# Six constants behind the first gates, three state copies on VectorE, and new delays in the planner of a two-layer macaron kernel

## The chip, the cores and the metric

The kernel runs on one core of a Trainium2 chip. A core has five engines with an instruction stream each: TensorE (PE; its weight loads are listed as PEld), VectorE (DVE), ScalarE (ACT), GpSimd (POOL) and SyncE (SP), which issues most of the transfers. Each engine runs its own instructions strictly in program order and waits for the others by semaphores. The metric is the device time of one execution in microseconds (us), lower is better.

## The reference

The input is x of 8 batches by 256 positions by 128 channels, 2048 tokens in all. The model is six residual steps, each on the layer norm of x:

```python
x = x + 0.5 * ffn0(layernorm(x))      # top 2 of 8 experts, 128 -> 512 -> 128, relu
x = x + attn0(layernorm(x))           # recurrence over 256 positions
x = x + 0.5 * ffn0(layernorm(x))      # the same experts again
x = x + 0.5 * ffn1(layernorm(x))      # 8 experts of 256, gelu, one expert for a token
x = x + attn1(layernorm(x))           # 16 heads, relu scores
x = x + 0.5 * ffn1(layernorm(x))
```

The recurrence of attn0 keeps an 8 by 8 state M for each batch and head (128 of them, one for each partition), with q and k scaled to unit length:

```python
out_t = einsum('bnh,bnhd->bnd', q_t, M)
delta = v_t - einsum('bnhd,bnd->bnh', M, k_t)
M = M + b_t * einsum('bnh,bnd->bnhd', k_t, delta)
```

Its output is divided by its root mean square, multiplied by rms_weight, and projected by Wo.

## The kernel before

**Tokens.** x lies in SBUF as 16 tiles of 128 tokens; a tile is 16 positions of all 8 batches. The first three steps run over five chunks of tiles, CHUNKS = (first tile, number): (0,3), (3,4), (7,4), (11,3), (14,2). So chunk 0 has 48 positions, chunks 1 and 2 have 64, chunk 3 has 48 and chunk 4 has 32.

**Calls of the first FFN.** There are eight, named by a pair: ("in",0) and ("in",1) for chunks 0 and 1, ("in",2) for the other nine tiles at once, and ("out",0) to ("out",4), which are the third step, a call for each chunk. ("in",0) and ("out",4) run every expert over all their tokens ("dense"); the rest are sorted. Below they are written in0 to in2 and out0 to out4; the profile joins names that differ in a number alone, so that pypin is the second projection of in1 and in2.

A call's path: `layer_norm` (L253; statistics on VectorE L259, reciprocal root on GpSimd L250, scaling on ScalarE L268); transposes on TensorE (ptg, L343) and gates (L323; logits plg, softmax with an exponential ex on ScalarE, the two best experts by VectorE, `both` L377). Then, for a sorted call, `route` (L423): TensorE counts the tokens of each expert (pcr, L444 and behind), VectorE makes each token's place (`slot`, L478) and each tile's expert (`tei`, L491), and `scattering` (L497) sends the rows to a buffer in DRAM, one indirect transfer by GpSimd for each tile and choice (L506): 18 for in2, 8 for out1. SyncE loads each tile's expert weights (`loading`) and fetches the sorted rows four tiles at a time (`fetching`, L714, xs). `experts` (L722) transposes them (ptp, L739), multiplies (ph, L793; py, L770), and stores the results as rows. `combining` (L813) gathers the rows for each token by GpSimd (yg, L864), weights them on ScalarE (dg, by half_ident), sums them on TensorE (pbc, L838 and L841) and adds them to x (L849). Before it TensorE turns the gates (pgb, L399).

**The scan.** `prepare` (L880) makes k, v, q and the rates of a chunk: layer norm, projections (pps, L929), activations (sps, L907), two transfers through DRAM that turn the layout (dts and ts), and `inverse` (L932), which squares on ScalarE (sqs, L937), sums on VectorE (sss, L940, sms, L944), takes the root (nrs, L947) and the reciprocal (nes, ris, L950 and L953). For each tile of the chunk it then copies v into the last column of a buffer of 16 states (M, L991, on ScalarE). `steps` (L1012) walks through the positions on VectorE in six instructions each (rk, L1054; u, L1059; e, L1032; Ms, L1064; r, L1068; mk, L1037). For each finished tile `finish` (L1080) multiplies states by q on GpSimd (qmo, L1094; q's own scaling, qns, is L1002) and sums on TensorE (pmo, L1100); once the chunk is done it turns the layout by DRAM (do, ot), takes the root mean square (pro, L1122; veo and rso, L247 and L250), projects by woT (pwo, L1130) and adds to x. A chunk's scan needs the state of the one before.

**What sets the order.** Nothing is scheduled by a compiler: each engine's program order is the order in which the class `Weave` (L43) emits. Streams (Python generators) say what they want next: an engine with an estimate of its time and the lag until its result is there, or a key that somebody has to mark. `Weave` keeps a time for each engine at which it is free, emits the earliest possible item (of items equally early the one of the higher rank) and moves the times on. A mark may be set later than now: `routed` (L511) is marked 2.5 us after the last scatter, `fetched` (L719) 3.0 us after its transfer's issue. An item of GpSimd between 1.25 and 1.35 us, that is a scatter or a gather, pushes VectorE's time back by 0.5 (L102). All these numbers act on the emitted order; at run time the engines wait for semaphores.

**Constants.** They are made before the streams start: half_ident (L139), part (L161 to L164, from two iotas), woT times rms_w (L207) and before (L215), six instructions on VectorE. half_ident is read by `combining`, before by `route`, woT by pwo, part by the second attention.

Of the kernel before, what the change touches and what calls it, by code (L numbers as in the profile page):

```python
# [17 lines left out]
P = 128  # L18
B, S, D = 8, 256, 128
NH, HD = 16, 8  # L20
E = 8
# [21 lines left out]
class Weave:  # L43
# [17 lines left out]
    def mark(self, key, us=None):  # L61
        self.done[key] = self.now if us is None else us
# [8 lines left out]
    def run(self, streams):  # L71
        for rank, s in streams:
            self.spawn(s, rank)
        streams, at, nexts = self.streams, self.at, self.nexts
        while any(n is not None for n in nexts):
            best = None
            for i, n in enumerate(nexts):
                if n is None:
                    continue
                if n[0] in self.free:  # L80
                    start = max(at[i], self.free[n[0]])
                elif n[0] == "until":
                    start = max(at[i], n[1])
                elif n in self.done:
                    start = max(at[i], self.done[n])
                else:
                    continue
                if best is None or (start, -self.ranks[i], at[i]) < best[:3]:
                    best = start, -self.ranks[i], at[i], i
            if best is None:  # L90
                raise RuntimeError([(st.__name__, n) for st, n in zip(streams, nexts) if n])
            start, _, _, i = best
            self.rank = self.ranks[i]
            if nexts[i][0] in self.free:
                engine, us, lag, table = nexts[i] + (None, None, LAGS[nexts[i][0]], None)[len(nexts[i]) :]
                if table and table != self.table:
                    self.load(table)
                    self.table = table
                    us += 1.3
                self.free[engine] = start + us  # L100
                if engine == "pool" and 1.25 < us < 1.35:
                    self.free["dve"] += 0.5  # L102
                start += us + lag
            at[i] = self.now = start
            nexts[i] = next(streams[i], None)
# [3 lines left out]
def kernel(ctx: ExitStack, tc: tile.TileContext, a: dict, out: bass.AP):  # L109
# [26 lines left out]
    ident = const.tile([P, P], F32, name="ident")  # L136
    make_identity(nc, ident)
    half_ident = const.tile([P, P], F32, name="half_ident")
    dve.tensor_scalar(half_ident, ident, 0.5, None, ALU.mult)  # L139
    ones = const.tile([P, P], F32, name="ones")  # L140
    pool.memset(ones, 1.0)
    mean_col = const.tile([P, 1], F32, name="mean_col")
# [15 lines left out]
    pool.iota(row, pattern=[[0, 4]], base=0, channel_multiplier=1)  # L158
    col = const.tile([P, 4], I32, name="col")
    pool.iota(col, pattern=[[1, 4]], base=0, channel_multiplier=0)  # L160
    dve.tensor_scalar(row, row, 3, 3, ALU.logical_shift_right, ALU.bitwise_and)  # L161
    part = const.tile([P, 4], F32, name="part")
    dve.tensor_tensor(part, row, col, ALU.is_equal)
    dve.tensor_scalar(part, part, QSCALE, None, ALU.mult)  # L164

    x1 = const.tile([P, NT, D], F32, name="x1")

# [9 lines left out]
    def slots_of(n, k=2):  # L177

        return (k * n * P + E * (P - 1)) // P
# [13 lines left out]
    def woven(dram, moe, pools):  # L193
# [5 lines left out]
        xd = dram.tile([B, S, D], F32, name="xd", tag="xd", bufs=1)  # L199
        n_f = F0 // P  # L200
        n_c = len(CHUNKS)
        tile_no = const.tile([P, slots_of(NT)], F32, name="tile_no")
        pool.iota(
            tile_no, pattern=[[1, slots_of(NT)]], base=0, channel_multiplier=0,
            allow_small_or_imprecise_dtypes=True,
        )
        dve.tensor_scalar(woT, woT, rms_w, None, ALU.mult)  # L207

        before = const.tile([E, 2, E], F32, name="before")
        pool.memset(before, 1.0)  # L210
# [1 line left out]
            out=before[:, 1, :], in_=before[:, 1, :], compare_op=ALU.is_ge, fill=0.0, base=0,  # L212
            pattern=[[1, E]], channel_multiplier=-1,
        )
        dve.tensor_scalar(before[:, 0, :], earlier[:E, :E], float(P), None, ALU.mult)  # L215


        calls = {("in", c): CHUNKS[c] for c in (0, 1)}
# [13 lines left out]
        for i in range(2):  # L232
            sorted_tiles[f"f{i}"] = slots_of(SORTED, 1)
            places[f"f{i}"] = 2 + i
            rooms.append(slots_of(SORTED, 1))

        def vec(n):

            return "dve", 0.07 + 0.00105 * n, 0.14

        SQRT, SILU, EXP, GELU = (f"{f}_and_others" for f in ("sqrt", "silu", "exp", "gelu"))

# [254 lines left out]
        def scattering(key, slots):  # L497
            c = chosen[key]
            n = sizes[key]
            yield "clear", places[key]  # L500

            views = dram_disjoint_views(dram_of[key][0], len(slots) * n)
            for i in range(n):
                for k in range(len(slots)):
                    yield "pool", 1.3, 0
                    pool.indirect_dma_start(  # L506
                        out=views.pop(),
                        out_offset=bass.IndirectOffsetOnAxis(ap=slots[k][:, i : i + 1], axis=0),
                        in_=c["xn"][:, i, :], in_offset=None,
                    )  # L510
            mark(("routed", key), weave.now + 2.5)  # L511

        def dram_rows(i, nt):

# [188 lines left out]
        def fetching():  # L703

            k = 0
            for key, nt in sorted_tiles.items():
                yield "routed", key
                for t in range(0, nt, TB):
                    if k >= XB:
                        yield "turned", k - XB  # L710
                    yield "sp", 0.4, 0
                    m = min(TB, nt - t)
                    xs = moe.tile([P, TB, D], F32, name=f"xs{k}", tag="xs", bufs=XB)
                    sync.dma_start(  # L714
                        out=xs[:, :m],
                        in_=dram_of[key][0][t * P : (t + m) * P].rearrange("(q p) d -> p q d", p=P),
                    )
                    sources[key, t // TB] = xs, m
                    mark(("fetched", key, t // TB), weave.now + 3.0)  # L719
                    k += 1  # L720

        def experts(key):  # L722
# [157 lines left out]
        def prepare(c):  # L880
# [104 lines left out]
            for i in range(n):  # L985
                if t0 + i >= MB:
                    yield "summed", t0 + i - MB
                yield "act", 0.35
                M = scan.tile([P, SL, HD, HD + 1], F32, name=f"M{name}_{i}", tag="M", bufs=MB)
                vs = v.rearrange("p h t -> p t h")[:, i * SL + 1 : min((i + 1) * SL + 1, ct)]  # L990
                act.copy(M[:, : vs.shape[1], :, HD], vs)  # L991
                states[t0 + i] = M
                mark(("room", t0 + i))
                if i == 0:
                    weave.spawn(queries(c, q, inverse))
# [10 lines left out]
        def scanning():  # L1006
            last = None
            for c in range(n_c):
                yield "room", CHUNKS[c][0]
                last = yield from steps(c, last)  # L1010

        def steps(c, last):  # L1012
# [33 lines left out]
            for t in range(ct):  # L1046
                if t and t % SL == SL - 1 and t + 1 < ct:
                    yield "room", t0 + t // SL + 1
                more = t + 1 < ct
                if more:  # L1050
                    yield "dve", 0.09, 0.0
                    rk = small.tile([P, HD], F32, name=f"rk{c}_{t}", tag="rk")
                    dot = small.tile([P, 1], F32, name=f"dot{c}_{t}", tag="dot")
                    dve.tensor_tensor_reduce(  # L1054
                        rk, r, kn[:, t + 1, :HD], 1.0, 0.0, ALU.mult, ALU.add, dot
                    )
                yield "dve", 0.14, 0.0
                u = small.tile([P, HD, HD], F32, name=f"u{c}_{t}", tag="u")
                dve.tensor_tensor(u, bc(kb[:, t], HD), bc_mid(r, HD), ALU.mult)  # L1059
                if more:  # L1060
                    yield "dve", 0.14, 0.0
                    e = e_of(t, mk)
                yield "dve", 0.13, 0.0
                dve.tensor_tensor(M(t + 1)[:, :, :HD], M(t)[:, :, :HD], u, ALU.add)  # L1064
                if more:
                    yield "dve", 0.08, 0.05
                    r = small.tile([P, HD], F32, name=f"r{c}_{t + 1}", tag="r")
                    dve.scalar_tensor_tensor(r, kb[:, t], dot, e, ALU.mult, ALU.add)  # L1068
                if t + 2 < ct:
                    yield "dve", 0.15, 0.0  # L1070
                    mk = mk_of(t + 1, t + 1)
                if t % SL == SL - 1:
                    mark(("states", t0 + t // SL))
            return end

        def finishing():
            for c in range(n_c):
                yield from finish(c)

        def finish(c):  # L1080
# [23 lines left out]
            yield "sp", 0.4, 2.8  # L1104
            do = dram.tile([P, HD, ct], F32, name=f"do{name}", tag=f"do{ct}")
            sync.dma_start(out=do, in_=o)
            yield "sp", 0.4, 2.8
            ot = scan.tile([P, BW], F32, name=f"ot{name}", tag="ot", bufs=1)
            ot = ot[:, : n * P].rearrange("p (b t) -> p b t", b=B)
            sync.dma_start(out=ot, in_=do.rearrange("(b n) d t -> (n d) b t", b=B))  # L1110
# [30 lines left out]

        def routing():
            for key in calls:
                if key[0] == "out":
                    yield "finished", key[1]
                    if key[1] > 1:
                        yield "x", ("out", key[1] - 2)
                yield from gates(key)
# [575 lines left out]
        def attended(b, sums):  # L1724
# [33 lines left out]
            for qc in range(2):  # L1758
# [16 lines left out]
        weave.run(  # L1775
            [
                (1, loading()), (1, fetching()), (1, routing()), (1, tensor()), (2, adds()), (2, combines()),
                (0, scanning()), (3, preparing()), (2, finishing()), (2, moving()), (1, clearing()),
                (1, opening()), (3, heads("f0")), (-1, everyone("f0")), (1, experts("f0")), (2, returning("f0")),
                (3, projecting()), (1, scoring()), (2, weighing()),  # L1780
                (3, heads("f1")), (-1, everyone("f1")), (1, experts("f1")), (2, returning("f1")), (1, storing()),
# [73 lines left out]
```

## Time and profile before

| | us |
|---|---|
| median of 9 runs | 871.78 |
| lowest to highest | 868.23 to 874.84 |
| profiled execution, its own time | 872.66 |
| its span, first to last instruction | 870.9 |
| mean granted TensorE clock | 0.889 |
| scan steps of chunk 0 | 99.3 to 147.3 |
| chunk 1 | 173.1 to 246.1 |
| chunk 2 | 254.8 to 325.5 |
| chunk 3 | 328.5 to 377.1 |
| chunk 4 | 380.9 to 422.2 |
| TensorE on in2's experts | 114.1 to 192.8 |
| TensorE on out1's experts | 314.8 to 363.5 |
| first tile of out2's experts | 403.5 |

The rows of chunks are the first and the last scan step on VectorE, with other instructions of VectorE between the steps. After out2 come out3, out4 and the second layer, some 450 us, in which TensorE leads most of the time.

The profile lists for each instruction its start from the beginning of the span, its duration, engine, line, operation and tiles; in square brackets stands the idle time of the engine just before it and what ended that. "POOL rsgin <- DVE vegin" is a wait of GpSimd for VectorE. The chain follows the work that ended last back to its releaser, piece by piece.

### The profile page before, as it was taken

To read this page: it belongs to the slowest core of one execution; us is meant where nothing else is said; L and a number is where in the kernel's file an instruction comes from. 1 tells how busy PE (TensorE), PEld (TensorE's weight loads), DVE (VectorE), ACT (ScalarE), POOL (GpSimd) and SP (SyncE) were. 2 spreads that over 40 slices of the span, in tenths; PEclk is the share of its full clock that TensorE was granted. 3 is DMA by queue.
4 is the path that set the end of the run, shared out by engine and by line. 5 is a ranking of instruction groups with operands and counts; after the bars stand their busy time and mean duration, and the time that the engine had idled before them with its cause. 6 is when DMAs were issued, how large, how long until landed. Compare 5 with 4: busy or idle time off the path is not lost.

```text
span 870.9 us, 17110 instructions
## 1 busy us (share of the span) xinstructions
PE 714.9 (82%) x5236; PEld 582.5 (67%) x5236; DVE 541.0 (62%) x3186; ACT 419.1 (48%) x1036; POOL 241.9 (28%) x337
## 2 busy tenths in 40 slices
PE   3999879986997558755999898995999999999581
PEld 2888868874586458744998786663955556666481
DVE  2434696398879999987501413768276876467721
ACT  3456737751476327512566444331566565554130
POOL 1041751017514430353323300003052332300303
PEclk9999979985699569866999997996999999999876
DMA  8075845605352455225495201005110000000522
GB/s 303 1 234 120 227 127 139 190 29 161 93 152 65 113 178 135 77 82 149 134 309 148 71 12 29 0 1 161 37 35 2 2 1 2 1 1 1 152 59 69
DMA packets 102842, 82.77 MB, mean 95 GB/s; under 512 B 38816, under 2 KB 82080, under 8 KB 102752
## 3 DMA queue, kind: packets, MB, share of 16 engines
q1 hardware_dynamic: 97840, 71.30, 28.4%
q0 software_dynamic: 4480, 9.18, 3.5%
q10 hardware_dynamic: 432, 1.20, 0.4%
q8 instruction: 43, 0.70, 0.3%
q14 instruction: 47, 0.39, 0.2%
HBM read 57.79 MB, written 23.86 MB: 94 GB/s over the span
## 4 chain that ended last, share of the span: by engine, by line
PE 53%; DVE 32%; DMA 4%; POOL 4%; issue 3%; ACT 3%; SPq 1%; POOLq 0%; ACTq 0%; DVEq 0%
PE ps L1665 4%; PE pa L1709 4%; DVE u L1059 4%; PE phpin L793 3%; DVE r L1068 3%; PE phf L1457 3%; DVE mk L1037 3%; PE pypin L770 3%; DVE Ms L1064 3%; PE pyf L1475 3%; PE phdin L664 3%; PE pypout L770 3%; PE phpout L793 3%; DVE e L1032 3%; PE pydin L674 2%
## 5 line engine op out<-in xcount | busy, mean ns | idle before, releaser
L1475 PEld LDWEIGHTS pyf<-w_W,hf 128*128 128x128 f32 x512 | 70.7, 200 | 24.9 <-issue 21.4
L1475 PE MATMUL pyf<-w_W,hf 128*128 128x128 f32 x512 | 76.0, 287 | 2.8 <-DVE x L1512 2.8
L797 ACT ACTIVATE hpout<-phpout,w 128x128 f32<-128x128 f32 x224 | 63.6, 372 | 30.0 <-PE phpout L793 26.5
L1464 ACT ACTIVATE hf<-phf 128x512 f32<-128x512 f32 x64 | 38.2, 597 | 64.9 <-PE phf L1457 64.9
L1457 PE MATMUL phf<-xTf,w_W 128*128 128x512 f32 x128 | 68.6, 621 | 0.0
L1059 DVE TENSOR_TENSOR u<-kbs,r 128x64 f32<-128x64 f32 x256 | 64.0, 250 | 0.2
L770 PE MATMUL pypout<-W,hpout 128*128 x448 | 60.4, 279 | 3.9 <-ACT hpout L797 3.9
L793 PE MATMUL phpout<-xTpout,w 128*128 128x128 f32 x448 | 60.3, 279 | 1.6 <-ACT xTpout L743 1.4
L1068 DVE SCALAR_TENSOR_TENSOR r<-kbs,dot,e 128x8 f32<-128x8 f32 x251 | 61.0, 243 | 0.0
L1037 DVE TENSOR_TENSOR mk<-Ms,kns 128x72 f32<-128x72 f32 x251 | 57.0, 227 | 5.5 <-ACT Ms L991 5.5
L770 PEld LDWEIGHTS pypout<-W,hpout 128*128 128x128 f32 x448 | 55.3, 194 | 4.7 <-ACT hpout L797 4.3
L1064 DVE TENSOR_TENSOR Ms<-Ms,u 128x64 f32<-128x64 f32 x251 | 57.3, 228 | 0.0
L793 PEld LDWEIGHTS phpout<-xTpout,w 128*128 128x128 f32 x448 | 55.5, 195 | 2.5 <-ACT xTpout L743 2.0
L797 ACT ACTIVATE hpin<-phpin,w 128x128 f32<-128x128 f32 x160 | 45.5, 378 | 18.4 <-PE phpin L793 12.8
L1032 DVE TENSOR_REDUCE e<-mk 128x8 f32<-128x72 f32 x251 | 53.5, 213 | 0.0
L1681 DVE TENSOR_SCALAR w<-ps 128x512 f32<-128x512 f32 x64 | 42.6, 683 | 15.7 <-PE ps L1665 15.4
L1094 POOL TENSOR_TENSOR qmo<-Ms,qns 128x1024 f32<-128x1024 f32 x16 | 32.0, 1999 | 67.0 <-DVE r L1068 50.0
L1100 PE MATMUL pmo<-qmo,ident 128*128 128x128 f32 x256 | 41.8, 332 | 6.2 <-POOL qmo L1094 6.0
L793 PE MATMUL phpin<-xTpin,w 128*128 128x128 f32 x320 | 45.5, 289 | 1.6 <-ACT sps L907 0.9
L1665 PE MATMUL ps<-q,k 32*128 32x256 f32 x512 | 45.4, 404 | 1.7 <-DVE w L1681 1.4
L1678 ACT ACTIVATE w<-ps 128x512 f32<-128x512 f32 x64 | 35.8, 596 | 22.5 <-PE ps L1665 22.1
L506 POOL DMA_INDIRECT rows<-xnf,slotrf x16 | 16.0, 997 | 109.2 <-DVE pastrf L482 104.9
(362 smaller groups left out, 1721.3 us busy)
## 6 DMA issues: line engine op xcount, KB each, us to landing
w<-in_w_dram SPq DMA_DIRECT2D x112, 258.0 KB, 3.4
xs<-rows SPq DMA_DIRECT2D x27, 256.0 KB, 3.6
rows<-x SPq DMA_DIRECT2D x5, 768.0 KB, 5.3
w<-in_w_dram SPq DMA_DIRECT2D x30, 128.0 KB, 2.5
rows<-ypout SPq DMA_DIRECT2D x12, 256.0 KB, 2.5
rows<-ypin SPq DMA_DIRECT2D x9, 256.0 KB, 2.3
W<-in_w_dram SPq DMA_DIRECT2D x8, 256.0 KB, 5.4
w_W<-in_w_dram SPq DMA_DIRECT2D x8, 256.0 KB, 4.8
```

The lines of the kernel that those rows point to most:

```text
L770: pe.matmul(py[:, t % TB, :], lhsT=h[:, g, :], rhs=of(e, g), start=g == 0, stop=g == n_f - 1)
L793: pe.matmul(ph[:, f, :], lhsT=first(w, f), rhs=xT[:, t % TB, :], start=True, stop=True)
L797: act.activation(h[:, f, :], ph[:, f, :], AF.Relu, bias=bias(w, f))
L1032: dve.tensor_reduce(e, mk, AX.X, ALU.add)
L1037: dve.tensor_tensor(mk, M(t), bc_mid(kn[:, t + 1], HD), ALU.mult)
L1059: dve.tensor_tensor(u, bc(kb[:, t], HD), bc_mid(r, HD), ALU.mult)
L1064: dve.tensor_tensor(M(t + 1)[:, :, :HD], M(t)[:, :, :HD], u, ALU.add)
L1068: dve.scalar_tensor_tensor(r, kb[:, t], dot, e, ALU.mult, ALU.add)
L1457: pe.matmul(ph, lhsT=l1["W"][:, e, f * P : (f + 1) * P], rhs=c["xT"][k], start=True, stop=True,)
L1475: pe.matmul(py[:, i, :], lhsT=before[0][ff][:, i * P : (i + 1) * P], rhs=second1(before[3], ff), start=ff == 0, stop=ff == n_f - 1,)
L1665: pe.matmul(pss[g][0][:, kc, :], lhsT=k[rows, j, kc * P : (kc + 1) * P], rhs=q[rows, :], start=True, stop=True,)
L1681: dve.tensor_scalar(w, ps, 0.0, None, ALU.max)
```

## The change

It has three parts.

1. The six constant instructions on VectorE leave the start. A new stream, `constants`, of rank 2 emits them once the gates of in0 have been emitted, and the routing waits for it before the gates of in1.
2. The copies of v into the state buffers of chunk 0, three of them, go to VectorE. Those of the other chunks stay on ScalarE.
3. Numbers of the planner: an indirect transfer pushes VectorE's time back by 0.8 instead of 0.5; routed is marked 4.0 after the last scatter instead of 2.5; fetched 4.5 after the issue instead of 3.0; the transfer of ot has a lag of 4.2 instead of 2.8; three of a scan step's six costs go from 0.13, 0.08 and 0.15 to 0.135, 0.1 and 0.17. The helper `vec` moves up so that the new stream can use it.

```diff
                 if engine == "pool" and 1.25 < us < 1.35:
-                    self.free["dve"] += 0.5
+                    self.free["dve"] += 0.8
...
-    dve.tensor_scalar(half_ident, ident, 0.5, None, ALU.mult)
...
-    dve.tensor_scalar(row, row, 3, 3, ALU.logical_shift_right, ALU.bitwise_and)
     part = const.tile([P, 4], F32, name="part")
-    dve.tensor_tensor(part, row, col, ALU.is_equal)
-    dve.tensor_scalar(part, part, QSCALE, None, ALU.mult)
...
-        dve.tensor_scalar(woT, woT, rms_w, None, ALU.mult)
...
-        dve.tensor_scalar(before[:, 0, :], earlier[:E, :E], float(P), None, ALU.mult)
+        def constants():
+
+            yield "gates", ("in", 0)
+            yield vec(E)
+            dve.tensor_scalar(before[:, 0, :], earlier[:E, :E], float(P), None, ALU.mult)
+            yield vec(P)
+            dve.tensor_scalar(half_ident, ident, 0.5, None, ALU.mult)
+            yield vec(P)
+            dve.tensor_scalar(woT, woT, rms_w, None, ALU.mult)
+            yield vec(4)
+            dve.tensor_scalar(row, row, 3, 3, ALU.logical_shift_right, ALU.bitwise_and)
+            yield vec(4)
+            dve.tensor_tensor(part, row, col, ALU.is_equal)
+            yield vec(4)
+            dve.tensor_scalar(part, part, QSCALE, None, ALU.mult)
+            mark(("constants",))
...
-            mark(("routed", key), weave.now + 2.5)
+            mark(("routed", key), weave.now + 4.0)
...
-                    mark(("fetched", key, t // TB), weave.now + 3.0)
+                    mark(("fetched", key, t // TB), weave.now + 4.5)
...
-                yield "act", 0.35
+                yield vec(SL * HD) if c == 0 else ("act", 0.35)
                 M = scan.tile([P, SL, HD, HD + 1], F32, name=f"M{name}_{i}", tag="M", bufs=MB)
                 vs = v.rearrange("p h t -> p t h")[:, i * SL + 1 : min((i + 1) * SL + 1, ct)]
-                act.copy(M[:, : vs.shape[1], :, HD], vs)
+                (dve.tensor_copy if c == 0 else act.copy)(M[:, : vs.shape[1], :, HD], vs)
...
-                yield "dve", 0.13, 0.0
+                yield "dve", 0.135, 0.0
                 dve.tensor_tensor(M(t + 1)[:, :, :HD], M(t)[:, :, :HD], u, ALU.add)
                 if more:
-                    yield "dve", 0.08, 0.05
+                    yield "dve", 0.1, 0.05
...
-                    yield "dve", 0.15, 0.0
+                    yield "dve", 0.17, 0.0
...
-            yield "sp", 0.4, 2.8
+            yield "sp", 0.4, 4.2
             ot = scan.tile([P, BW], F32, name=f"ot{name}", tag="ot", bufs=1)
...
+                if key == ("in", 1):
+                    yield ("constants",)
...
-                (0, scanning()), (3, preparing()), (2, finishing()), (2, moving()), (1, clearing()),
+                (0, scanning()), (3, preparing()), (2, constants()), (2, finishing()), (2, moving()), (1, clearing()),
```

In the order that comes out each engine has the instructions it had, but for the three copies and for three more loads of ScalarE's activation tables (23 instead of 20): two around the exponential of in2's gates, one around that of out1's.

## The prediction

> **What bounds the kernel now.** I read the page's shares and its chain first, then the timelines of the engines that the moved work touches, then the stretch in which TensorE stands still.
>
> ```profile
> PE 714.9 (82%) x5236; PEld 582.5 (67%) x5236; DVE 541.0 (62%) x3186; ACT 419.1 (48%) x1036; POOL 241.9 (28%) x337
> PE 53%; DVE 32%; DMA 4%; POOL 4%; issue 3%; ACT 3%; SPq 1%; POOLq 0%; ACTq 0%; DVEq 0%
> ```
>
> TensorE and VectorE share the path: TensorE through the experts, VectorE through the scan, and they hand over by gathers and scatters on GpSimd (POOL). So what counts is which instruction stands ahead of which on each engine; nothing is added but three VectorE instructions in ScalarE's stead, and three table loads.
>
> **The start.** VectorE's timeline opens with the constants:
>
> ```profile
> 8.40 0.29 DVE L207 TENSOR_SCALAR w_rows<-w_rows 128x128 f32<-128x128 f32 x1 [8.40 <-DMA w_rows<-in_rows_dram]
> ...
> 9.28 0.15 DVE L215 TENSOR_SCALAR before<-earlier 8x8 f32<-8x8 f32 x1
> 9.36 0.28 DVE L259 BATCH_NORM_STATS2 stgin<-x 128x6 f32<-128x128 f32 x1
> ```
>
> The first statistics stand behind L207, whose rows land at 8.40, though ScalarE's first table load at 4.05 is released by x itself. With the six constants gone they start at 4.05: gain 9.36 − 4.05 = 5.3 us. TensorE, whose transposes follow, is busy 30.0 of 30 us from 20 to 50, so it hands the gain on; w1, which the first expert matmul at 15.71 needs, landed at 9.05 and would be needed at 10.4. Bounds: 0, if a weight is late, to 5.3; I take 5.3. The constants themselves (0.96 us) go behind the first gates.
>
> **State copies.** L991 takes 432 ns on ScalarE. On VectorE no such copy exists; a 128x1 copy (L1356) takes 149 ns, a 128x256 one (L1641) 421, and the nearest, 128x128 (L1329), 291. Three are 0.4 to 1.3 us, and I take 0.8 on VectorE against up to the 1.92 that it waited for ScalarE's copy before chunk 0. Neither counts: after chunk 0 the scan stands still for its next input.
>
> ```profile
> 147.37 1.87 DVE L1064 TENSOR_TENSOR end<-Ms,u 128x64 f32<-128x64 f32 x1
> 159.85 0.69 DVE L940 TENSOR_REDUCE sss<-sqs 128x64 f32<-128x512 f32 x1 [10.61 <-ACT sqs L937]
> 246.27 0.68 DVE L940 TENSOR_REDUCE sss<-sqs 128x64 f32<-128x512 f32 x1
> ```
>
> The last line is chunk 2's norm: the squares it waits for ended at 244.07, so 2.2 us of slack lie there.
>
> **Planner numbers.** They issue nothing, but the whole order is built from them. Going through the new order engine by engine with the old durations, these moves matter.
>
> (a) The sorted tokens of in2. Chunk 0's sums, sms, nes and ris stand ahead of slotrin2 on VectorE, its matmuls pcrin2 stand later on TensorE, and exgin2 is behind two sps activations and one table load on ScalarE. On the old clock the slots come at 92.0 instead of 85.3: +6.7. Bounds: 3.4 (the three norm instructions and the activations alone) to 10.
>
> (b) GpSimd. Eighteen scatters (L506) run one by one, then eight gathers ygcin1 (L864):
>
> ```profile
> 85.31 1.03 POOL L506 DMA_INDIRECT rows<-xngin,slotrin  x1 [16.12 <-DVE terin L488]
> ...
> 108.30 0.96 POOL L506 DMA_INDIRECT rows<-xngin,slotrin  x1 [0.30 <-issue]
> 109.56 0.99 POOL L864 DMA_INDIRECT ygcin<-rows,slotrin  x1 [0.30 <-issue]
> ```
>
> In the new order the last four scatters stand behind all eight gathers. At 109.56 − 108.30 = 1.26 each that is +10.1. qns0 stands five scatters earlier, ahead of its input; I take 1.7 for that wait (0 to 3). The chain shows who waits:
>
> ```profile
> 108.30 2.27 DMA rows<-xngin,slotrin
> ...
> 110.64 3.44 DMA xs<-rows
> 114.07 0.04 issue
> 114.12 1.13 PE ptpin L739 x4
> ```
>
> All of in2's experts wait for the last scatter. Together 6.7 + 10.1 + 1.7 − 5.3 = +13.2: ptpin2_0 at 127.3 instead of 114.1.
>
> (c) TensorE around it. Moved ahead of that transpose, into the wait: pgbin1, two pbcin1 and pmo0_0, 6.9 us. Moved in before in2's last matmul: pmo1_0 and pmo1_1, 3.6. A new wait for out0's gate sums: 4.0 (0 to 6.5, the wait that pcrout had), while the old 3.4 at that place and 2.0 of small waits go. Sum −6.9 + 3.6 + 4.0 − 3.4 − 2.0 = −4.7. So in2's last matmul ends 13.2 − 4.7 = 8.5 late.
>
> (d) From there to the scan. A second out0 scatter stands ahead of gathers ygcin2 (+1.3), so chunk 2's tokens are +9.8, and after the 2.2 of slack the scan of chunk 2 starts +7.6. Chunk 1, whose preparation moves well ahead, starts some 10 us earlier, which gains nothing while chunk 2 waits for tokens. From chunk 2 on the scan carries the 7.6.
>
> (e) out1 and out2. slotrout1 moves six steps earlier (step 26 of chunk 2 instead of 32); at 0.77 us a step out1's tiles start 4.6 earlier against the scan, 310.2 on the old clock. But the eight gathers ygcout1 now stand ahead of rsgout2:
>
> ```profile
> 356.83 1.01 POOL L250 TENSOR_TENSOR rsgout<-vegout,minus_half 128x4 f32<-128x4 f32 x1 [6.11 <-DVE vegout L247]
> ...
> 367.99 1.05 POOL L864 DMA_INDIRECT ygcout<-rows,slotrout  x1 [0.17 <-issue]
> ```
>
> The gathers need out1's rows. out1's matmuls took 314.84 to 363.5, 48.7 us; without pwo2, pmo3_0 (3.3) and a wait of 3.5 for the last relu they end at 310.2 + 41.9 = 352.1; rows stored 2.9 later; gathers 10.1; then rsgout2: done at 366.1. VectorE wants it at 359.9 (offgout2, step 32 of chunk 3 in both orders). So the scan may stall 6.2, 9.7 if the relu's wait stays, or nothing if the rows come early. I take the middle of 0 and 9.7: +4.9. Then out2's slots stand six scan steps later (+4.6), rso3 in the middle of its scatters (+0.9), and pmo4_0, ptgout3 and plgout3 (3.7) run in TensorE's wait before out2 instead of in it: +1.8. After out2's middle TensorE's order is the old one.
>
> **Sum.** 7.6 + 4.9 + 1.8 = +14.3 against the profiled execution's 872.7: 887.0. That execution is 0.9 above the median of the nine runs, 871.8, so 886.
>
> **Two rules weighed, beside the sum.** Table loads: the trace's cost 1283 ns each, three more 3.8 us on an engine at 48%, covered by waits; the next activation follows 10 ns after a load. The Trainium skill ("ScalarE: Activation LUTs", section "What ACT_TABLE_LOAD costs") puts a drain of some 1380 ns on top, so three would be 8.0 us by it: it speaks against this change, but the trace shows no such drain, and I leave both out of the sum.
>
> While TensorE stood still its clock was granted less (columns: us, PE, PEld, DVE, ACT, POOL busy, granted clock, DMA share, GB/s):
>
> ```profile
> 100.00:110.00 10.00, 5.16 (x47) 4.97 (x45) 9.55 (x78) 4.36 (x15) 7.74 (x9) 0.90 0.75 206
> 110.00:120.00 10.00, 5.21 (x23) 4.56 (x24) 10.00 (x72) 2.00 (x7) 8.15 (x8) 0.50 0.52 152
> ```
>
> It was 0.50 from 108.0 to 121.7, 7.6 us into the work again: 3.8 us lost. "TensorE: Matmul & The Clock Gate" ("Part 1: The HAM clock gate") says that one idle window of about 3.4 us halves the rate and as much steady work restores it; by that the longer pause costs about the same once, by the row 3.8 once. In the sum it stays as it was.
>
> **The rivals.**
>
> R1, faster: the start gain carries. If GpSimd's slots come early enough that ptpin2_0 runs by 112.6 and out1's rows come early enough for rsgout2, the rest of the sum (−1.5 to there, −4.7, +1.3, −2.2, +1.8) gives −5.3, the start's own gain: 871.8 − 5.3 = 866. For it: a TensorE that hands on every early microsecond, its shortened stage, a chunk 1 that starts earlier. Against: the ten microseconds of gathers in a queue that is full, as its 0.30 us gaps show. By the same terms it turns where ptpin2_0 comes at 117.9.
>
> R2, no change: (a) at its lower bound (−3.3), no wait of qns0 (−1.7), none of out0's gate sums (−4.0) and none at offgout2 (−4.9): 886 − 13.9 = 872. Each is possible, all four together are not likely, though one early start of the scatters would help three of them.
>
> R3, much slower: the same queue at its worst. rsgout2 with the full stall of 9.7 (+4.8), and in2's slots at the upper bound (+3.3): 886 + 8 = 894. It needs out1's tail unshortened.
>
> R4: the numbers do not do what they say, that is, later marks move order alone and the transfers land as before (xs in 3.2 us median, scatter in 2.27). That is true of every mark, and is why no gain is put down to them: it is a part of each case.
>
> **How the numbers follow.** Main case 0.47 (878 to 890 as its own range), R1 0.26, R2 0.13, R3 0.14. Changes under 0.3%, 2.6 us, cannot be told from none. Faster: R1 and a little of R2, 0.28; same: most of R2, 0.09; slower 0.63. The range goes from 863, R1 with 3 more from the earlier chunk 1, to 893, just under R3.
>
> **What would show it.** bn_stats at about 4.1; the first slotrin2 scatter after 85 and four scatters behind the gathers; ptpin2_0 near 127; chunk 2's scan starting near 262; an idle stretch on VectorE at offgout2 of about 5; out2's scatters some 14 later than 385.8. If ptpin2_0 comes before 118, or the stall at offgout2 is absent while chunk 2 starts no later than 255, the forecast is wrong.

## The result, and the profile after

| | before | after |
|---|---|---|
| median, us | 871.78 | 892.93 |
| lowest to highest | 866.79 to 875.82 (31 runs) | 891.23 to 897.08 (10 runs) |
| span of the profiled execution | 870.9 | 892.1 |
| mean granted TensorE clock | 0.889 | 0.874 |

The change makes the kernel slower: ratio 1.025, 95% interval 1.0228 to 1.0273. The forecast had 886 and the direction; but the way there differs, and its second half was not foreseen. Setting each milestone of the two traces side by side shows it (start of the first, end of the last instruction, us):

| milestone | before | after | forecast shift | measured shift |
|---|---|---|---|---|
| first statistics | 9.4 | 4.1 | -5.3 | -5.2 |
| in2's slots (end of slotrin2) | 84.5 | 85.3 | +1.4 | +0.8 |
| in2's first transposes | 114.1 | 127.3 | +13.2 | +13.2 |
| in2's last matmul | 192.8 | 197.7 | +8.5 | +4.9 |
| first step of chunk 2's scan | 254.8 | 258.0 | +7.6 | +3.2 |
| out2's first transposes | 403.5 | 415.9 | +18.0 | +12.4 |
| out2's last matmul | 444.9 | 451.3 | +14.3 | +6.5 |
| first expert matmul of f0 | 519.4 | 533.5 | +14.3 | +14.1 |
| first scores of the second attention | 630.6 | 645.0 | +14.3 | +14.4 |
| first expert matmul of f1 | 746.6 | 768.8 | +14.3 | +22.2 |

So of the 21 us some 3 are there when chunk 2's scan begins, 6.5 at out2's end, 14.4 when the attention begins, and 22 when it is over. Between f0 and the attention, where TensorE's order is the same in both traces, the shift stays (14.1 and 14.4). Lines of after are 12 higher than those of before from the new stream on, 14 in the second layer, and in the kernels with a recorded order higher again. GpSimd's timeline of after around in2:

```profile
86.06 1.11 POOL L518 DMA_INDIRECT rows<-xngin,slotrin  x1 [22.45 <-DVE pastrin L494]
...
97.70 1.13 POOL L1014 TENSOR_TENSOR qns<-ts,ris 128x384 f32<-128x384 f32 x1 [1.66 <-DVE mk L1049]
...
106.81 0.98 POOL L876 DMA_INDIRECT ygcin<-rows,slotrin  x1 [0.49 <-issue]
...
115.60 0.94 POOL L876 DMA_INDIRECT ygcin<-rows,slotrin  x1 [0.30 <-issue]
116.85 1.00 POOL L518 DMA_INDIRECT rows<-xngin,slotrin  x1 [0.30 <-issue]
...
120.69 0.96 POOL L518 DMA_INDIRECT rows<-xngin,slotrin  x1 [0.30 <-issue]
```

Eight gathers stand between the fourteenth and the last four scatters, and qns0 waits 1.66 us. TensorE's timeline shows what was done in the pause and when in2 begins:

```profile
109.51 0.77 PE L853 MATMUL pbcin<-ygcin,dgcin 128*128 128x128 f32 x2 [5.34 <-DMA ygcin<-rows,slotrin]
...
123.70 3.78 PE L1112 MATMUL pmo<-qmo,ident 128*128 128x128 f32 x16 [4.67 <-POOL qmo L1106]
127.28 1.06 PE L751 MATMUL ptpin<-ident,xs 128*128 128x128 f32 x4
129.01 2.05 PE L805 MATMUL phpin<-xTpin,w 128*128 128x128 f32 x16 [0.67 <-ACT xTpin L755]
```

The windows over in2's experts, before's first, then after's (columns as in the prediction):

```profile
114.12:192.80 78.68, 72.59 (x540) 66.62 (x540) 57.73 (x402) 52.00 (x152) 16.99 (x13) 0.91 0.45 123
```

```profile
127.28:197.70 70.42, 65.42 (x530) 61.47 (x530) 66.65 (x495) 49.55 (x146) 11.22 (x7) 0.97 0.46 129
```

in2 takes 8.3 us less. A part of it is work that was moved into the pause, another the clock, 0.97 instead of 0.91: of in2's stretch 13.8 us ran at 0.50 in before and 4.8 in after. Work at half clock now lies in the pause, ahead of in2 (pmo0_0 took 3.78 us for 16 matmuls there, against 1.95 in before).

The late stretch, on GpSimd, VectorE and TensorE of after:

```profile
498.75 0.94 POOL L876 DMA_INDIRECT ygcout<-rows,slotrout  x1 [0.30 <-issue]
499.71 2.04 POOL L262 TENSOR_TENSOR rsf<-vef,minus_half 128x4 f32<-128x4 f32 x2
```

```profile
500.79 0.36 DVE L1300 TENSOR_SCALAR xnf<-x,mvf,rsf 128x128 f32<-128x128 f32 x1 [6.34 <-POOL rsf L262]
501.05 0.35 DVE L707 SCALAR_TENSOR_TENSOR x<-pydout,gategout,x 128x128 f32<-128x128 f32 x1
```

```profile
501.45 2.07 PE L686 MATMUL pydout<-W,hdout 128*128 128x128 f32 x8 [4.19 <-DVE x L707]
```

The roots rsf00 and rsf01 of the second layer's first norm run behind all six gathers ygcout3; in before they ran behind four, at 491.02. VectorE takes its work in order, so the sums of the dense out4 (L707) wait behind the norm that needs rsf, and TensorE waits 4.19 us for a bank, a piece of the memory that it writes to, that these sums free. In before TensorE waited there too, for xnf, but 2.69 us. The windows show the clock behind it, before's first:

```profile
490.00:500.00 10.00, 7.01 (x34) 6.04 (x35) 3.46 (x13) 1.69 (x4) 5.05 (x5) 0.83 0.11 28
500.00:510.00 10.00, 10.00 (x73) 8.81 (x73) 1.97 (x6) 5.08 (x13) 0.00 (x0) 1.00 0.08 17
```

```profile
500.00:510.00 10.00, 8.55 (x33) 7.63 (x34) 3.11 (x12) 1.94 (x5) 1.75 (x2) 0.53 0.03 8
510.00:520.00 10.00, 10.00 (x49) 9.03 (x49) 1.68 (x5) 2.62 (x6) 0.00 (x0) 0.61 0.09 20
```

With the clock at 0.61 TensorE looks busy for all of the ten microseconds and does 49 matmuls, where before's does 73 at 1.00. Over the whole way from out2's last matmul to the first of f0, before's first:

```profile
444.87:519.42 74.55, 68.47 (x499) 62.30 (x498) 14.85 (x70) 41.97 (x117) 18.62 (x87) 0.98 0.40 125
```

```profile
451.34:533.47 82.13, 74.30 (x498) 67.67 (x497) 14.68 (x70) 42.23 (x117) 18.50 (x87) 0.90 0.35 101
```

Of the 7.6 us 5.8 are TensorE's own time for the same matmuls and 1.8 its idle time. Its clock was 0.50 for 17.1 us of that way, in before for 3.4; half of the difference, 6.8 us, is an estimate of what the clock cost.

### The profile page after: what moved, and what is told of

Same layout as the page of the kernel before. It is cut to its first block, busy times and chain, and to the rows that moved or that the text cites. A ratio compares the mean times of both kernels' runs of the same rounds, so it can differ in the third digit from the quotient of the medians.

```text
span 892.1 us, 17122 instructions
## 1 busy us (share of the span) xinstructions
PE 723.9 (81%) x5236; PEld 586.8 (66%) x5236; DVE 536.4 (60%) x3189; ACT 423.6 (47%) x1036; POOL 241.0 (27%) x337
## 4 chain that ended last, share of the span: by engine, by line
PE 49%; DVE 29%; POOL 7%; issue 6%; ACT 4%; DMA 4%; SPq 0%; POOLq 0%; DVEq 0%; ACTq 0%
DVE x L1526 4%; PE ps L1679 4%; PE pa L1723 3%; PE phf L1471 3%; PE phdin L676 3%; PE phpout L805 3%; PE pmo L1112 3%; PE pypout L782 3%; DVE u L1071 3%; PE pyf L1489 3%; PE pydin L686 2%; PE pypin L782 2%; DVE mk L1049 2%; DVE Ms L1076 2%; PE phpin L805 2%
## 5 line engine op out<-in xcount | busy, mean ns | idle before, releaser
L1112 PE MATMUL pmo<-qmo,ident 128*128 128x128 f32 x256 | 45.1, 349 | 22.2 <-POOL qmo L1106 17.1
L1071 DVE TENSOR_TENSOR u<-kbs,r 128x64 f32<-128x64 f32 x256 | 60.6, 237 | 0.1
L1112 PEld LDWEIGHTS pmo<-qmo,ident 128*128 128x128 f32 x256 | 42.5, 259 | 24.8 <-POOL qmo L1106 18.5
L1080 DVE SCALAR_TENSOR_TENSOR r<-kbs,dot,e 128x8 f32<-128x8 f32 x251 | 57.0, 227 | 0.0
L809 ACT ACTIVATE hpin<-phpin,w 128x128 f32<-128x128 f32 x160 | 45.5, 374 | 17.1 <-PE phpin L805 12.4
L1066 DVE CUSTOM_DVE_ANT_0 rk<-r,kns 128x8 f32<-128x8 f32 x251 | 45.7, 182 | 0.1
## 6 DMA issues: line engine op xcount, KB each, us to landing
w<-in_w_dram SPq DMA_DIRECT2D x112, 258.0 KB, 3.6
```

What stands on the lines that cost most here:

```text
L809: act.activation(h[:, f, :], ph[:, f, :], AF.Relu, bias=bias(w, f))
L1112: pe.matmul(pm, lhsT=ident, rhs=qm[:, :, h, :], start=h == 0, stop=h == HD - 1)
```

## The experiments

All ran on chips where the kernel before takes 921 to 928 us, not 872, and where the whole change costs less. So each is read by its ratio to before on the same chip, and the traces by differences inside one trace, or between traces of these chips. The two theories are set out anew for each experiment. The first chip, where the loss is 2.5%, saw none of these runs.

**Parts of the change, each in the order that the planner makes of it.** e1: part 1 alone. e2: part 2 alone. e3: part 3 alone.

> The six constants alone behind the first gates; copies and planner numbers as before. Theory 1 (all of the loss comes from the order that the new planner numbers bring): the first statistics start at 4.1 instead of 9.4, the order stays near the old one, 866 to 871 us. Theory 2 (the edits themselves cost, by VectorE work pushed into the routing of in1): 873 or more, with in2's transposes later than 114.

Measured: 0.9823 (0.9796 to 0.985), 16 us, three times the start's 5.3 and more than theory 1 had.

> The three state copies of chunk 0 alone on VectorE. Theory 1: the scan of chunk 0 starts 1 to 2 us earlier and stands still after it, as before: 871 to 873 us. Theory 2 (the freed ScalarE and the changed planner state move the order enough to cost): 875 or more.

Measured: 1.0005 (0.9983 to 1.0028).

> The planner's numbers alone, constants and copies as before. Theory 1: all of the loss and a little more, since the start gains nothing: 890 to 900 us. Theory 2 (the loss is of the edits): 868 to 876 us.

Measured: 1.0014 (0.9987 to 1.0041). The parts do not add: 0.9823, 1.0005 and 1.0014 alone, and 1.0066 together (e8). Each part gives an order of its own (e2's is close to the old one, e1's and e3's differ from it in many places), so a part's ratio holds for its own order alone. Theory 1 as it was put for e3, that the numbers carry all of the loss in any case, fell.

**The edits without a new order (e4).** The planner's choice is replaced by a recorded list of which stream comes next; the list is that of the kernel before, with the constants inserted behind the first gates.

```diff
-        while any(n is not None for n in nexts):
...
+        todo = list(ORDER)
+        while todo:
+            for j, name in enumerate(todo):
+                i = self.names.get(name)
+                n = None if i is None else nexts[i]
+                if n is not None and (n[0] in self.free or n[0] == "until" or n in self.done):
+                    break
...
+            todo.pop(j)
```

> Constants moved and copies on VectorE, as in the change, but every engine's order is the old one, replayed from a recorded list. Theory 1: the start's 5.3 us are gained and kept in part; 865 to 870 us. Theory 2: 872 or more.

Measured: 0.9946 (0.993 to 0.9962), 0.54% or 5.0 us of 926. On TensorE and GpSimd the trace has before's order without a difference. So on this chip constants and copies cost nothing, the start's gain of 5 us arrives whole, and what the change loses is order: the new numbers stand in e4's code too.

**New order up to a point, old from there (e8, e5 to e7).** The list is the change's own up to an item, then what is left in the old sequence.

> The whole change once more, beside the next three and beside before on the same chip, since before took 926 us where the first four ran and 872 where the change was measured. If the change's cost is the order's alone (theory 1), its ratio to before is 1.025 again, 893 us against 872. If it hangs on how fast that chip delivers instructions and transfers (theory 2), the ratio is near 1.0 wherever before takes 926.

> The change's code; the order of all engines is the new one until the planner reaches the first step of chunk 2's scan, and the old one from there. Theory 1 (each stretch of the new order adds its own loss): the 3.2 us by which chunk 2's scan was late and hardly more, 872 to 877 us where before takes 872. Theory 2 (the early delay is what costs, and what follows only magnifies it, by a clock that has fallen or transfers that collide): 888 or more.

> As the one before, but the new order reaches until the first item of out3's experts. Theory 1: 6.5 us, the lateness of out2's last matmul, so 876 to 881 us where before takes 872, since the stretch with rsf00 behind six gathers and the attention run in the old order. Theory 2: 888 or more.

> As the one before, but the new order reaches until the first scores of the second attention. Theory 1: 14.4 us, the lateness of the first scores, so 883 to 889 us where before takes 872; the 7 us that the attention adds in the new order are gone. Theory 2: 891 or more.

| new order until | ratio | interval |
|---|---|---|
| chunk 2's scan (e5) | 0.9852 | 0.9815 to 0.9888 |
| out3's experts (e6) | 0.9921 | 0.9895 to 0.9946 |
| first scores (e7) | 0.9990 | 0.9958 to 1.0021 |
| the end (e8) | 1.0066 | 1.0033 to 1.0099 |

e8 has neither theory's number; what the chip changes is told below. Each stretch adds: 6.4, 6.4 and 7.0 us of 921, where the two first traces have 3.3, 7.9 and 7.8. That speaks for theory 1: an early delay that only grows would have shown in e5. e5, e6 and e7 all came out below the number of theory 1. On these chips the new order gains up to chunk 2 (0.9852 against e4's 0.9946, 8.7 us, and 13.6 against before), where on the first chip it was 3.2 us late against before: the 17 us between these two are about the difference between 1.025 and 1.007.

**Single moves in the change's order.** Each changes the place of a few GpSimd instructions, f3 also of some on TensorE and ScalarE. The whole change did not run on their chip; it has 1.0066 in e8 and 1.0077 in h1.

> The whole change in its own order, but for one move on GpSimd: rsgout2 runs ahead of the eight gathers ygcout1 instead of behind them. Theory 1 (the prediction's step e: the scan stalls at offgout2 for the gathers): 2 to 6 us less than the whole change, so a ratio of 1.000 to 1.005 where the whole change has 1.0066, and 1.018 to 1.023 where it has 1.025. Theory 2 (what follows out2 is set by its slots six scan steps later and not by the stall): within 1.5 us of the whole change.

Measured: 1.0104 (1.0057 to 1.0150), a loss against the whole change's 1.0066 and 1.0077 that neither theory had, though the intervals overlap. GpSimd now waits for VectorE's statistics before it gathers:

```profile
384.17 1.37 POOL L326 TENSOR_TENSOR rsgout<-vegout,minus_half 128x4 f32<-128x4 f32 x1 [6.40 <-DVE vegout L323]
385.71 1.05 POOL L940 DMA_INDIRECT ygcout<-rows,slotrout  x1 [0.18 <-issue]
```

The gathers start 11.9 us behind out1's last matmul (373.8); in e8 it is 4.8 (368.3 to 373.1). This trace is 5 us later than e8's at chunk 3's first step, before the move acts, and 10.6 at its last. I read it so that the gathers ahead of the norm are the better order once TensorE's order has the sums ahead of out2's transposes, and that the move undid half of a pair; TensorE's half was not tried with it.

> The whole change in its own order, but rsf00 and rsf01 run ahead of the last two gathers ygcout3, as they did before. Theory 1 (these two gathers make TensorE wait, its clock falls, and the stretch out3 to the first scores loses 6 to 8 us by it): 4 to 8 us less than the whole change, a ratio of 0.998 to 1.002 where the whole change has 1.0066. Theory 2 (the clock would fall all the same, by the old wait for xnf00): 0 to 3 us less.

Measured: 1.0049 (1.0019 to 1.0078), by the ratio a gain of 1.6 us against e8 with intervals that overlap: theory 2's number, not theory 1's. Its trace, of the fastest of its runs (925.5; the median is 931.7), is clear in the place that it changes: TensorE's wait for L771 (the same sum) and its windows, then those of h1, the whole change:

```profile
530.12 1.16 PE L750 MATMUL pydout<-W,hdout 128*128 128x128 f32 x8 [0.92 <-DVE x L771]
```

```profile
520.00:530.00 10.00, 8.13 (x54) 6.83 (x53) 4.58 (x32) 5.24 (x14) 5.49 (x6) 1.00 0.32 98
530.00:540.00 10.00, 9.88 (x70) 9.05 (x71) 3.74 (x14) 4.25 (x10) 2.57 (x3) 1.00 0.11 26
```

```profile
522.00:532.00 10.00, 6.77 (x46) 5.58 (x44) 3.67 (x28) 4.79 (x13) 6.54 (x7) 0.91 0.19 54
532.00:542.00 10.00, 9.03 (x35) 8.12 (x36) 3.11 (x12) 2.11 (x5) 1.26 (x2) 0.50 0.02 6
```

Two gathers fewer ahead of rsf make the wait 0.92 instead of 3.35 us, and the clock does not fall there. From out2's last matmul to the first of f0 it takes 78.4 us, in e8 90.5, in h1 87.1, with 6.8, 27.3 and 23.9 us of it at 0.50.

> The whole change in its own order, but in2's last four scatters run ahead of the eight gathers ygcin1, and TensorE does in2's first transposes and first matmuls ahead of in1's sums. Theory 1 (the prediction's step b, the gathers ahead delay in2 by 10.1 us): in2's first transposes 8 to 10 us earlier, its last matmul 2 to 4 earlier since the moved sums go back between its tiles, the total 2 to 4 us less than the whole change. Theory 2 (chunk 2's scan is bound elsewhere): no change within 1.5 us.

Measured: 1.0125 (1.0077 to 1.0172). in2's transposes do come 13.5 earlier than in e8, and its last matmul 6.6 later:

```profile
125.60:216.10 90.50, 81.85 (x573) 74.55 (x573) 74.82 (x563) 52.47 (x154) 20.84 (x16) 0.86 0.40 109
```

90.5 us for in2, against 70.4 in e8 (139.1 to 209.4). The pause stands empty (13.7 us), so the half clock falls on in2's own tiles (24.9 us at 0.50, in e8 4.3), and in1's sums go back between them. Theory 1, that the gathers ahead of the scatters are the loss, fell on these chips: with the sums in the pause that order is no worse.

> The change's code in the old order until the first scores of the second attention, and in the new order from there. Theory 1 (the attention's new order costs some 7 us by itself, whatever comes before): the old order throughout had 0.9946 of before, so 1.001 to 1.004 here. Theory 2 (the attention lost time only because it was entered late or at another clock): 0.993 to 0.997.

Measured: 1.0033 (1.0009 to 1.0057), against e4's 0.9946: 8 us by the attention's order alone. From the first scores to f1 it takes 133.4 us here; in e4, with the old order, 124.3. The clock has a large share in this: 20.5 us of the stretch are at 0.50 here, 6.8 in e4, which by half makes 6.8 of the 9.1 us.

**Together, and once more (h1 to h4).**

> The whole change again, as the partner of the next three on the same chip. Theory 1 (the loss behind chunk 2 is 18 us wherever it runs, and only the stretch before chunk 2 differs with the chip): ratio 1.003 to 1.012 where before takes 920 or more, 1.025 where it takes 872. Theory 2 (the loss is another on every chip): outside of these.

Measured: 1.0077 (1.0042 to 1.0112), as theory 1 has it for such a chip.

> The six constants alone behind the first gates, again. Theory 1 (the gain of 1.8% is of the order that the planner makes, and holds): ratio 0.978 to 0.987 where before takes 920 or more, 0.990 to 0.998 where it takes 872, that is the start's 5.3 us and little else. Theory 2 (it was an accident of one chip): 0.99 to 1.0 where before takes 920.

Measured: 0.9822 (0.9776 to 0.9868), the same as e1 on another chip.

> The new order until the first scores of the second attention, but with rsf00 and rsf01 ahead of the last two gathers ygcout3, and the old order from there. Theory 1 (the two losses are separate and add): 7 us less than the whole change by the attention and 4 to 10 less by rsf, together 11 to 17 less, a ratio lower by 0.012 to 0.018 than that of the whole change of this call. Theory 2 (one hangs on the other): 5 to 10 us less.

Measured: 0.9936 (0.9900 to 0.9971), 0.0141 below h1: the two late losses add, 13 us together. Beside e7, whose order on TensorE, VectorE, ScalarE and GpSimd differs from h3's in the place of rsf00 and rsf01 alone, it is 0.0054 lower, 5 us; f2 had 1.6. So rsf's place is worth some 2 to 5 us here, with intervals that overlap.

> The change's code in the new order until the first step of chunk 2's scan, and from there in the order of the kernel with the constants alone. Theory 1 (early gain and later order add): where before takes 920 or more, 0 to 4 us less than the constants alone; where it takes 872, 5 to 9 more than these, since there the new order reaches chunk 2 3.2 us late instead of some 5 early.

Measured: 0.9872 (0.9827 to 0.9916), 4.6 us above h2, where theory 1 had it below: the two orders do not add at this seam. The best version found is the constants alone, 1.8% faster than before on these chips. On the first chip it was not run.

## Why the prediction was right in direction and wrong in its account

**The start.** Right: 4.12, gain 5.2. It was handed on to in2's routing, and e4 has 5 us of it at the end.

**(a) and (b), in2's rows.** Right in the place and nearly in the numbers: slots +0.8 where the terms 6.7 and -5.3 give +1.4, four scatters behind the gathers, 1.66 us of wait at qns0, transposes at 127.3. What it was taken to cost is not confirmed: f3, which takes those gathers out of the way and lets in2 begin first on TensorE, was no faster, though on another chip and with TensorE's order changed too.

**(c), in2's stretch on TensorE.** Mis-sized: -4.7 forecast, -8.3 measured. The term left out was the clock, which the prediction held to be the same ("In the sum it stays as it was"). With the sums and pmo0_0 in the pause the slow microseconds fall on them: 9.0 us fewer of in2 ran at 0.50, by half 4.5, which is more than the missing 3.6.

**(d).** +3.2 at chunk 2's scan instead of +7.6, which follows from (c) within 1 us.

**(e).** The gathers do stand ahead of rsgout2, and offgout2 waits for it, but 1.6 us instead of 4.9: out1's matmuls ended at 352.3, where the sum had 352.1 on the old clock, 359.7 with the 7.6. out2's scatters are 10.7 later, not "some 14". Its first transposes are 12.4 late, where the terms 7.6, 4.9, 4.6 and 0.9 give 18.0; its block then takes 35.4 us instead of 41.3 (3.7 of these 5.9 were in the sum), so that 6.5 are left at its end.

**The step that failed** is the sentence "After out2's middle TensorE's order is the old one", and with it a sum that ended there. The order is not the old one: on TensorE it differs again in out3 and out4, is the same in f0's experts, and differs through the second attention; the engines around it differ too. The clock, which the sum left as it was, failed with it: 17.1 us at 0.50 on the way to f0 instead of 3.4. What the runs put in the step's place: 7.9 us between out2's end and the first scores (e7 against e6 has 6.4), and 7.8 in the attention (e8 against e7, f4). The two gathers ahead of rsf00 and the fallen clock are a cause of the first part, some 2 to 5 us by the ratios of f2 and h3; that they are all of it is not shown. That the total came near the forecast is a cancelling, so luck: 8 us too much up to out2, and 15 too little behind it.

In the attention the trace shows scores that TensorE meets before VectorE has freed their bank:

```profile
656.28 0.70 PE L1679 MATMUL ps<-q,k 32*128 32x256 f32 x4 [0.73 <-ACT q L1647]
658.58 2.07 PE L1679 MATMUL ps<-q,k 32*128 32x256 f32 x12 [1.59 <-DVE w L1695]
```

TensorE's waits for w before ps sum to 4.1 us there and to 1.4 in before, and its clock was 0.50 from 657.7 to 664.5, in before's stretch never. From the first scores to f1, before's first:

```profile
630.55:746.63 116.08, 110.00 (x1230) 67.72 (x1229) 82.50 (x268) 68.88 (x147) 39.25 (x51) 1.00 0.03 8
```

```profile
644.96:768.80 123.84, 112.25 (x1230) 68.34 (x1229) 84.45 (x269) 68.49 (x146) 40.83 (x53) 0.97 0.03 7
```

TensorE is 5.5 us longer idle and 2.3 longer busy with as many matmuls. The waits for w named above are 2.7 of these 5.5, those of poa, which turns the attention's output, for its input `on` (2.5 against 0.7) another 1.8. That the waits and the clock go away with these few places was not tried.

**The rivals.** R1 and R2 did not come: they needed early slots, which did not come, and none of them looked behind out2. R3 named the stall at offgout2 and in2's slots; neither was at its worst. R4, that the new numbers move order alone, is what e4 shows.

**What stays open.** Why the kernel before takes 921 to 928 us on the later chips. The trace of e2, whose ratio is 1.0005, shows TensorE without work and without a releaser in in1's experts, where before has no such gap:

```profile
103.33 2.08 PE L770 MATMUL pypin<-W,hpin 128*128 x8 [8.61 <-issue]
```

ScalarE stood still at the same time:

```profile
102.91 1.14 ACT L797 ACTIVATE hpin<-phpin,w 128x128 f32<-128x128 f32 x4 [8.91 <-remote]
```

SyncE, which issues the weight loads, has no instruction from 93.5 to 102.9, between its second and third load of that time; GpSimd went on with its scatters. What held the three is not in the trace. e4, with the old order, has such a gap of 7.33 us at that place, e5 and e8, with the new one, 4.03 and 4.48 (for hpin). It may be why the new order gains on these chips; this was not tried.

## What to carry to other kernels

Where a planner makes the whole program order, a small edit is three changes: the edit, the new order near it, and a new order of everything behind. Replaying the old order under the new code measures the first by itself, and changing from one order to the other at a few points says in which stretch the rest lies. Compare both orders up to the last instruction before a delay is carried to the end unchanged, and look behind each wait of TensorE for what the clock does after it.

## What was not expected of the hardware

The clock's fall can cost more than the wait that brings it, and the wait's length does not tell how much. In after a wait of 4.19 us, ended at 501.45, is followed by a granted clock of 0.50 until about 517.8, although TensorE is busy all the time: 16 us at half speed, some 8 lost. In about the same place a wait of 2.69 us is followed by 3.4 us at 0.50 in before and by 13.7 in e8, one of 3.35 by 17.1 in h1, and one of 0.92 in f2 left the clock at 1.00. After the pause of in2 the clock came back 7.5 us into the work in before, in after about 5 (123.7 to 128.6). The Trainium skill ("TensorE: Matmul & The Clock Gate", section "Part 1: The HAM clock gate") gives one or more busy windows of about 3.4 us for the way back; the 16 us of this case are far longer than one such window, and the measurement decides. Why TensorE needed so long there stays open.
